# Value projections from a second, interleaved copy of the tokens, one transfer per chunk, and the second norm on ScalarE

## The chip, the cores and the metric

The kernel runs on one core of a Trainium2 chip. A core has a matrix engine (TensorE, PE in the profile; PEld is its weight load), a vector engine (VectorE, DVE), an activation engine (ScalarE, ACT), a general engine (GpSimd, POOL) and a sequencer that here issues nearly all DMA transfers (SyncE, SP). Each has its own instruction queue and works through it in order; semaphores join them. The metric is the device time of one execution in microseconds, as the median of several runs.

## The reference

The input is x with 32 sequences of 128 tokens of 128 features. First comes a cross-attention with 16 query heads of 8 features and 4 key/value heads, whose keys and values come from a context and whose scores get a bias from the time between tokens. Its result is added to x. Then x is normalized once and goes through six layers, whose result is added again. One layer is:

```
def attn_layer(x, Wqkv, qs, ksc, Wo):
    q, k, v = split(x @ Wqkv)            # 16 heads of 64 features
    q = l2norm(q) * qs;  k = l2norm(k) * ksc
    q, k = rotary(q), rotary(k)          # with a scale that depends on the position
    out = local_attention(q, k, v)       # windows of 32 tokens, each sees itself and the one before
    return out @ Wo

def ffn_layer(x, g, bln, W1, b1, W2, b2):
    xn = (x - mu) / sqrt(var + 1e-05) * g + bln
    a, gate = split(xn @ W1 + b1)
    return a * gelu(gate) @ W2 + b2

x = attn_layer(shift_tokens(x), ...) + x
x = ffn_layer(shift_tokens(x), ...) + x
```

`shift_tokens` replaces half of a token's features by those of the token before it. The "second norm" of the title is the layer norm that opens the feed-forward part; the norm of q and k is the L2 norm.

## The kernel before

**Units and groups.** A unit is one sequence in one layer: its 128 tokens lie on 128 partitions. Four sequences make a group (`GB = 4`), so a layer has 8 groups and 32 units, and six layers have 48 groups and 192 units. The groups of a layer do not depend on each other. Before the layers, `xgroup` and `xunit` compute the cross-attention, also in 8 groups of 4.

**What a group does.** `lgroup` transposes the shifted tokens of a group on TensorE (`ax`) and splits them into a rounded half and a remainder (`axh` on ScalarE, `axl` on VectorE), `xh` and `xl`. A product of two float32 matrices is made of three matmuls of such halves (`split3`, L435 to L437). Then come four units, and `ffn` ends the group.

**What a unit does.** For each of four chunks of 512 columns (q has two, k has two), `qk` projects, `sq` squares on ScalarE, `tab` multiplies by the rotary tables on VectorE (L793), `ss` sums the squares (L816), and `add` joins the rotary halves on GpSimd (L809). `newton` makes 1/sqrt of the 32 norms of a token: a maximum (`dmx`, L396), Ln and Exp on ScalarE, and one Newton step, which squares the estimate (L405) and multiplies twice (L409, L415), all `dnw` on VectorE. `mul` scales on GpSimd (L834), `tq` transposes, `evq` copies out (L838).

**The values.** Wv and Wo of a head are multiplied together beforehand (`mp`, `mh`, `ml` in `prep`), so the value projection `y` gives, for every head, 128 features that only have to be weighted and summed. `y` makes four chunks of 512 columns (4 heads of 128). `yt` copies a chunk out of PSUM (L851). The attention needs the keys of one window on 32 partitions, with the four windows and the heads along the free dimension, and one chunk's heads on their own 32 partitions. So for each chunk c, four transfers `dm` (L861), one per window u, move partitions 32u to 32u+31 of `yt` to partitions 32c to 32c+31 of `ysh`, columns 512u to 512u+511, 64 KB each. `av` (L913) multiplies with the transposed weights.

**The attention between.** `msk` writes the mask into PSUM (L884), `sc` adds the scores (L879), `mx` takes the negated row maximum (L892), `fold` adds it by a matmul (L893), `ex` exponentiates into `pr` (L895), `sm`, `rl` and `pl` normalize (L896 to L898), `pt` transposes blocks (L900).

**The second norm.** `ffn` adds the attention to x (L921), starts the token shift (`psh`, two transfers on SP, L752), takes mean and variance (`st`, `ag`), and `newton` makes 1/sqrt with its small operations on GpSimd. Then `xn` subtracts the mean and scales on VectorE, one instruction for each of the four sequences (L939). `ptn` transposes, and the gated feed-forward follows.

**The order of the work.** The order of each engine's queue is fixed when the program is built. Every operation is a `Sched.op` with a name; the table `COST` gives its engine, how long it holds the engine and when its result is ready; `LATER` adds to its priority (larger is later, in units of sequences), and `KEEP` says how many of the five shared PSUM banks must stay free behind it. `Sched.run` plays the program through with these durations: whenever an engine is free, it takes the ready operation with the smallest priority for which buffers can be had. Buffers come from pools of fixed size: for instance three `yt`, two `ysh`, two pairs `xh`/`xl`, three `pr`, and six `S` for the scores of the cross-attention, four of them borrowed from a `ysh` (`NS = 2` adds two). Options (`YD`, `ADD`, `XN`) choose between ways that are both written out; those taken move values inside SBUF, add on GpSimd and normalize on VectorE.

Of the kernel before, what the change touches and what calls it, by code (L numbers as in the profile page):

```python
# [8 lines left out]
F32 = mybir.dt.float32  # L9
# [7 lines left out]
P = 128  # L17
# [6 lines left out]
NYD = 6  # L24
NS = 2
YD = "sb"
ADD = "pool"
XN = "dve"
# [6 lines left out]
    mxs=("POOL", .26, .30), dmx=("DVE", .17, .25), dnw=("DVE", .18, .25), ln=("ACT", .2, .24), ep=("ACT", .2, .24), nw=("POOL", .31, .34),  # L35
    mul=("POOL", 1.08, 1.1), tq=("PE", .45, .70), evq=("ACT", .5, .62), evk=("ACT", .5, .62),
    y=("PE", .69, .90), yt=("ACT", .5, .62), dm=("SP", .62, 2.3), dw=("SP", .62, 3.5), dr=("SP", .62, 4.5),
# [3 lines left out]
    eps=("POOL", .22, .26), lnf=("ACT", .22, .21), epf=("ACT", .22, .21), nwf=("POOL", .3, .34), xn=("DVE", 1.05, 1.13), xn2=("POOL", 1.08, 1.1),  # L41
# [13 lines left out]
LATER = dict(y=3, xtr=0.75, ptn=1.5, fold=0.35, qk=-0.5, xsc=-1, axh=-1, evk=-0.25, ss=0.25, sc=0.25, sq=0.5, um=0.75,  # L55
    axl=-1.5, tq=1.25, xev=1.75, mul=0.75, mx=-1, evq1=-1.0, tab0=0.25, lnb=0.5, um1=-1, xpj=0.75, yt1=-1.5, rl1=0.75,
    dw=-1, gel=0.75, xn1=1, nw=-0.25, msk0=2, yt3=-1.25, ta3=0.5, pwm=-0.4, ag=0.25, tq0=1.5, pa0=-0.5, dnw=1, io=0.6,
    xnh=1.5, ep=-1.5, mx1=0.25, pt1=1.5, adda=0.9, ex1=1, gel1=0.35, dr=-0.15, ta1=1.5, msk=-1.5, adda1=2, xo=1.5,
    ta0=0.5, sm0=2.85, xsb=3, rl0=-1, mx0=-1, wve=-1.5, um0=0.25, evq2=-1.5, tq1=0.5, add3=2.1, xnl=2, gate1=0.5,
    nwf=1, xn2=0.25, add=1.5, lof=-1.5, yt2=0.5, wvp=0.75, ta=-0.5, xn=-0.5, ldw=-0.25, tq2=-0.25, res2=0.35, pt=0.25,  # L60
    xat=2)

KEEP = dict(qk=1, y=1, gate=1, pa=3, xtr=0, xpj=0, pv=1, td=1, xsc=0, wvp=2, mp=2, bip=2, sc0=0, ax=0, tq=0)
# [159 lines left out]
def body(ctx: ExitStack, tc: tile.TileContext, x, ctx_in, fside, mask_in, xWq, xWk, xWv, xWo, xtw,  # L223
         Wqkv, q_scale, k_scale, Wo, ln_g, ln_b, W1, b1, W2, b2, cst, x1d, y2d, out):
# [27 lines left out]
    if ADD == "dma":  # L252
        pool("rt", 5, [P, 1024])
    else:
        pool("rt", 10, [P, 512])
    pool("qT", 4, [P, 512])
    pool("ysh", 2, [P, 2048])
    pool("yt", 3, [P, 512], inorder=False)
    pool("pr", 3, [P, 512])
    pool("PT", 3, [P, 512])  # L260
    pool("xh", 2, [P, GB, P], F32R)
    pool("xl", 2, [P, GB, P], F32R)
    pool("nh", 1, [P, 512], F32R)
# [38 lines left out]

    S.pool("yd", [y2d[i] for i in range(y2d.shape[0])], False)
# [79 lines left out]
    def newton(names, pri, V, src, n, floor, eps, pool_, cols):  # L383
        v, y, t = [Buf(p) for p in pool_]

        def sl(b):
            return b.t[:, 0:n]
# [16 lines left out]
        def f3():  # L404
            e.tensor_tensor(sl(t), sl(y), sl(y), op=ALU.mult)  # L405
# [18 lines left out]
        S.op(names[3], f3, pri, [y], [t])  # L424
# [182 lines left out]
    def xgroup(g):  # L607
# [66 lines left out]
        if ADD == "dma":  # L674
            two = [Buf("rt", dt=F32R), Buf("rt", dt=F32R)]
            qs = [(two[t // 2], t % 2 * 512) for t in range(4)]
        else:
            qs = [(Buf("rt", dt=F32R), 0) for t in range(4)]
# [77 lines left out]
    def lgroup(l, g, w):  # L756
# [8 lines left out]
             [lo])  # L765
        for j in range(GB):
            unit(l, g, j, w, G, base + j)
        ffn(l, g, w, G, base + GB - 1)

    def unit(l, g, j, w, G, pri):  # L770
# [4 lines left out]

        hs = [(Buf("rt"), Buf("t")) for _ in range(2)] if ADD == "dma" else None

        def proj(c):
            pp, sq = Buf("pj"), Buf("sq")
            rt, t = hs[c // 2] if hs else (Buf("rt"), Buf("t"))  # L780
            o = c % 2 * 512 if hs else 0
            tok = Buf(None, 0) if hs else rt
            rts.append((rt, o, tok))
# [13 lines left out]
            def ta():  # L797
                nc.vector.tensor_tensor(rt.t[:, o:o + 512].rearrange("p (h d) -> p h d", d=64),
                                        pp.t.rearrange("p (h d) -> p h d", d=64), bc(tab.t[:, c // 2, 0], 8), op=ALU.mult)

            def tb():
                nc.vector.tensor_tensor(
                    t.t[:, o:o + 512].rearrange("p (h s d) -> p h s d", s=2, d=32)[:, :, ::-1, :],
                    pp.t.rearrange("p (h s d) -> p h s d", s=2, d=32),
                    bc(tab.t[:, c // 2, 1].rearrange("p (s d) -> p s d", s=2), 8), op=ALU.mult)

# [4 lines left out]
            if hs:  # L811
                S.op("ta", ta, pri, [pp, tab], [rt], also=[t], k=c)
                S.op("ta", tb, pri, [pp, tab], [t], k=c)
            else:
                S.op("tab", tab2, pri, [pp, tab], [t], k=c)
            S.op("ss", lambda: nc.vector.tensor_reduce(ss.t[:, c * 8:(c + 1) * 8], sq.t.rearrange("p (h d) -> p h d", d=64),  # L816
                                                       axis=AX.X, op=ALU.add), pri, [sq], [ss], k=c)
            if not hs:
                S.op("add", add, pri, [t], [rt], k=c)
            elif c % 2:  # L820
                S.op("adda", lambda: nc.gpsimd.dma_start(rt.t, t.t, accum_op=ALU.add), pri, [t, rt],
                     [rt, *(x[2] for x in rts[-2:])], k=c)
# [4 lines left out]
        for c in range(4):  # L827
            def tr(c):
                (rt, o, tok), pt, d = rts[c], Buf("pj"), Buf("qT")
                qT.append(d)  # L830

                def mul():
                    rv = rt.t[:, o:o + 512].rearrange("p (h d) -> p h d", d=64)
                    nc.gpsimd.tensor_tensor(rv, rv, rn.t[:, c * 8:(c + 1) * 8].unsqueeze(2).to_broadcast([P, 8, 64]),  # L834
                                            op=ALU.mult)
                S.op("mul", mul, pri, [tok, rn], [tok], also=[rt], k=c)
                S.op("tq", lambda: tr4(pt.t, [rt.t[:, o + k * P:o + (k + 1) * P] for k in range(4)]), pri, [tok], [pt], also=[rt, d], k=c)
                S.op("evq", lambda: nc.scalar.copy(d.t, pt.t), pri, [pt], [d], k=c)  # L838
            tr(c)
# [3 lines left out]
        yds = [Buf("yd"), Buf("yd")]  # L843
        for c in range(4):
            def yy(c):
                py, yt = Buf("pj"), Buf("yt")
                mh, ml = w["m"][c]
                yd = yds[c // 2]
                S.op("y", lambda: split3(py.t, (xh.t[:, j, :], xl.t[:, j, :]), (mh.t, ml.t)), pri, [xh, xl, mh, ml], [py],
                     also=ysh, k=c)  # L850
                S.op("yt", lambda: nc.scalar.copy(yt.t, py.t), pri, [py], [yt], k=c)  # L851
                if YD == "dram":
                    S.op("dw", lambda: nc.sync.dma_start(yd.t[:, c % 2], yt.t), pri, [yt], [yd], k=c)
                    if c % 2:
                        r = slice(32 * c - 32, 32 * c + 32)
                        S.op("dr", lambda: nc.sync.dma_start(
                            ysh[0].t[r].rearrange("p (u n) -> p u n", u=4),
                            yd.t.rearrange("u c i n -> (c i) u n")), pri, [yd], ysh, k=c)
                else:
                    for u in range(4):  # L860
                        S.op("dm", lambda u=u: nc.sync.dma_start(ysh[0].t[32 * c:32 * c + 32, u * 512:(u + 1) * 512],  # L861
                                                                 yt.t[32 * u:32 * u + 32, :]), pri, [yt], ysh, k=c)
            yy(c)
# [55 lines left out]
    def ffn(l, g, w, G, pri):  # L919
# [15 lines left out]

        if XN == "dve":
            def xnf():
# [128 lines left out]
```

## Time and profile before

| | us |
|---|---|
| median of 3 runs | 3436.73 (3434.03 to 3436.86) |
| profiled execution, device time | 3450.15 |
| its span, first to last instruction | 3448.4 |
| TensorE busy | 3113.7 |
| VectorE busy | 2917.7 |
| ScalarE busy | 2227.7 |
| GpSimd busy | 2413.6 |

The mean granted TensorE clock was 0.972. The profiled execution was 13.4 us longer than the median, so a sum made on the profile is compared with 3450.15 first. A row of the profile names the line of the kernel, the engine, the operation, the tiles written and read, how many there were and how long they were busy; a wait is named after the work that released it. Matmuls overlap in their pipeline, and their ends are modelled, so a busy TensorE may still have room. "SPq" is SyncE's queue, whose issues do not count as busy.

### The profile page before, as it was taken

To read this page: it belongs to the slowest core of one execution; us is meant where nothing else is said; L and a number is where in the kernel's file an instruction comes from. 1 tells how busy PE (TensorE), PEld (TensorE's weight loads), DVE (VectorE), ACT (ScalarE), POOL (GpSimd) and SP (SyncE) were. 2 spreads that over 40 slices of the span, in tenths; PEclk is the share of its full clock that TensorE was granted. 3 is DMA by queue.
4 is the path that set the end of the run, shared out by engine and by line. 5 is a ranking of instruction groups with operands and counts; after the bars stand their busy time and mean duration, and the time that the engine had idled before them with its cause. 6 is when DMAs were issued, how large, how long until landed. Compare 5 with 4: busy or idle time off the path is not lost.

```text
span 3448.4 us, 118846 instructions
## 1 busy us (share of the span) xinstructions
PE 3113.7 (90%) x47887; PEld 2404.7 (70%) x47887; DVE 2917.7 (85%) x6115; ACT 2227.7 (65%) x4415; POOL 2413.6 (70%) x2470
## 2 busy tenths in 40 slices
PE   8877899898799999799999999999999999999997
PEld 5554677676576777577777777777777777777775
DVE  5556998889678998779999889998899988899984
ACT  6766666666466666566766666666666667676664
POOL 6546877677557777656777767777677777677773
PEclk9998999999899999899999999999999999999998
DMA  4200132323133333233233333332332333333332
GB/s 105 58 13 10 48 78 67 76 68 90 41 87 74 74 80 76 56 92 74 69 79 79 87 77 78 75 82 68 91 80 69 79 74 85 79 75 87 82 78 71
DMA packets 253765, 251.06 MB, mean 73 GB/s; under 512 B 127486, under 2 KB 148258, under 8 KB 253218
## 3 DMA queue, kind: packets, MB, share of 16 engines
q1 hardware_dynamic: 252786, 243.12, 28.8%
q8 instruction: 380, 6.23, 0.9%
q14 instruction: 167, 1.37, 0.1%
q10 hardware_dynamic: 432, 0.34, 0.0%
HBM read 25.24 MB, written 4.19 MB: 9 GB/s over the span
## 4 chain that ended last, share of the span: by engine, by line
PE 34%; DVE 26%; DMA 11%; SPq 11%; ACT 10%; issue 6%; POOL 2%; ACTq 0%; POOLq 0%; DVEq 0%
SPq L861 10%; PE bank__68 L913 7%; DMA xt<-xt 2%; PE bank__66 L879 2%; PE bank__64 L441 1%; PE bank__67 L879 1%; PE bank__63 L441 1%; PE bank__61 L441 1%; PE bank__65 L441 1%; PE bank__63 L435 1%; PE bank__62 L435 1%; PE bank__62 L441 1%; PE bank__65 L435 1%; PE bank__61 L435 1%; PE bank__63 L436 1%
## 5 line engine op out<-in xcount | busy, mean ns | idle before, releaser
L884 ACT COPY bank__66<-mask 128x512 f32<-128x512 f32 x192 | 117.0, 610 | 5.7 <-PE bank__66 L362 4.4
L884 ACT COPY bank__67<-mask 128x512 f32<-128x512 f32 x192 | 116.5, 607 | 1.5 <-PE bank__67 L362 1.1
L724 ACT ACTIVATE ysh__88<-ysh__88 128x512 f32<-128x512 f32 x96 | 60.7, 634 | 57.0 <-POOL ysh__88 L722 56.9
L961 ACT ACT_TABLE_LOAD x48 | 61.6, 1283 | 0.9
L241 ACT ACT_TABLE_LOAD x48 | 61.6, 1283 | 0.9
L921 DVE TENSOR_TENSOR xt<-bank__68,xt 128x512 f32<-128x512 f32 x48 | 33.0, 687 | 16.7 <-PE bank__68 L913 16.5
L441 PE MATMUL bank__61<-cs,ysh__88 128*128 128x128 f32 x84 | 15.5, 315 | 10.2 <-ACT ysh__88 L724 10.2
L441 PE MATMUL bank__63<-cs,ysh__88 128*128 128x128 f32 x80 | 14.6, 312 | 10.8 <-ACT ysh__88 L724 10.5
L441 PEld LDWEIGHTS bank__63<-cs,ysh__88 128*128 128x128 f32 x80 | 9.9, 156 | 15.0 <-ACT ysh__88 L724 12.8
L441 PEld LDWEIGHTS bank__61<-cs,ysh__88 128*128 128x128 f32 x84 | 10.9, 160 | 13.6 <-ACT ysh__88 L724 12.2
L441 PE MATMUL bank__62<-cs,ysh__88 128*128 128x128 f32 x76 | 14.5, 324 | 5.6 <-ACT ysh__88 L724 5.4
L441 PE MATMUL bank__64<-cs,ysh__88 128*128 128x128 f32 x68 | 12.7, 318 | 7.6 <-ACT ysh__88 L724 7.5
L441 PE MATMUL bank__65<-cs,ysh__88 128*128 128x128 f32 x76 | 13.3, 302 | 6.4 <-ACT ysh__88 L724 6.1
L441 PEld LDWEIGHTS bank__62<-cs,ysh__88 128*128 128x128 f32 x76 | 10.7, 168 | 8.4 <-ACT ysh__88 L724 7.6
L695 DVE TENSOR_TENSOR xt<-bank__68,xt 128x512 f32<-128x512 f32 x8 | 5.5, 685 | 12.8 <-PE bank__68 L693 12.8
L441 PEld LDWEIGHTS bank__64<-cs,ysh__88 128*128 128x128 f32 x68 | 8.6, 159 | 10.9 <-ACT ysh__88 L724 10.2
L441 PEld LDWEIGHTS bank__65<-cs,ysh__88 128*128 128x128 f32 x76 | 9.5, 154 | 9.5 <-ACT ysh__88 L724 8.7
L991 POOL TENSOR_TENSOR raw__50988<-raw__50988,xt 128x512 f32<-128x512 f32 x1 | 1.3, 1262 | 19.7 <-DVE xt L984 19.7
L718 DVE CUSTOM_DVE_ANT_0 ysh__88<-bank__63,rt__2156 128x128 f32<-128x128 f32 x12 | 2.8, 287 | 12.7 <-ACT S__90 L727 6.2
L727 ACT COPY ysh__88<-bank__63 128x512 f32<-128x512 f32 x20 | 11.9, 597 | 1.8 <-PE bank__63 L441 1.6
L727 ACT COPY ysh__88<-bank__61 128x512 f32<-128x512 f32 x21 | 12.3, 586 | 1.2 <-PE bank__61 L441 1.1
L718 DVE CUSTOM_DVE_ANT_0 ysh__88<-bank__61,rt__2550 128x128 f32<-128x128 f32 x12 | 2.8, 288 | 12.1 <-ACT S__90 L727 5.6
(24588 smaller groups left out, 15904.7 us busy)
## 6 DMA issues: line engine op xcount, KB each, us to landing
xt<-xt SPq DMA_DIRECT2D x96, 112.0 KB, 2.5
xt<-in_x SPq DMA_DIRECT2D x16, 128.0 KB, 3.2
x_scratch<-xt SPq DMA_DIRECT2D x8, 256.0 KB, 3.0
xt<-xt SPq DMA_DIRECT2D x96, 15.0 KB, 2.2
stg__750<-in_L_ffn_Wo SPq DMA_DIRECT2D x1, 512.0 KB
stg__1904<-in_L_ffn_Wo SPq DMA_DIRECT2D x1, 512.0 KB
stg__20461<-in_L_ffn_Wo SPq DMA_DIRECT2D x1, 512.0 KB
stg__28190<-in_L_ffn_Wo SPq DMA_DIRECT2D x1, 512.0 KB
```

What stands on the lines that cost most here:

```text
L241: S.back = lambda: nc.scalar.preload_act_table_set("natural_log_exp_and_others")
L435: nc.tensor.matmul(pt, lh, rh, start=True, stop=False)
L436: nc.tensor.matmul(pt, lh, rl, start=False, stop=False)
L441: nc.tensor.transpose(dst[:, k * P:(k + 1) * P], srcs[k], ident)
L724: S.op("xex", lambda: nc.scalar.activation(sm.t, sm.t, AF.Exp), pri, [sm], [sm], table="E")
L727: S.op("xev", lambda: nc.scalar.copy(sm.t, pt.t), pri, [pt, sm], [sm])
L861: S.op("dm", lambda u=u: nc.sync.dma_start(ysh[0].t[32 * c:32 * c + 32, u * 512:(u + 1) * 512], yt.t[32 * u:32 * u + 32, :]), pri, [yt], y ...
L879: nc.tensor.matmul(s4[a][32 * c:32 * c + 32, half, wd, lo:64], q[r, c * P + 32 * wd:c * P + 32 * wd + 32], k[r, c * P + 32 * wd - 32 + lo: ...
L884: S.op("msk", lambda b=b: nc.scalar.copy(b.t, mask), pri, (), [b], k=a)
L913: nc.tensor.matmul(po.t[32 * wd:32 * wd + 32, j * P:(j + 1) * P], p5[a][:, half, wd, blk, :], ysh[0].t[:, u * 512 + h * P:u * 512 + (h + 1 ...
L921: S.op("res", lambda: nc.vector.tensor_tensor(xv(g), hv(po.t), xv(g), op=ALU.add), pri, [po, X[g]], [X[g]])
L961: S.op("gel", lambda: nc.scalar.activation(u.t[0:n], pg.t[0:n], AF.Gelu, bias=b1c.t[0:n, 1, i:i + 1]), pri, [pg, b1c], [u], table="G", k=i)
```

## The change

After `axh` and `axl` of a group, two more ScalarE copies (`xph`, `xpl`) write the same two halves into a second pair of buffers, `xq`, with the tokens in another order: token 32u + i goes to column 4i + u. The value projections take `xq` as their stationary operand in place of `xh` and `xl`, so that `yt` has token 32u + i on partition 4i + u. Four neighbouring partitions then hold what one partition of `ysh` needs, and one transfer of 256 KB moves a chunk, with 128 rows read and 32 rows written. The matmuls are as many as before and of the same shape.

The second norm is one ScalarE activation per sequence, with the scale 1/sqrt and a bias of minus mean times 1/sqrt, which a new small VectorE operation (`nmr`) writes over the mean. In the norm of q and k the square of the Newton step goes from VectorE to ScalarE (`ysq`).

To make room, `S` loses one buffer (`NS` is 1) and `pr` one (2 for 3); `xq` has two buffers, which is one pair. All of `LATER` is new, `KEEP` differs in `pa`, `xtr` and `ax`, and `COST` books `dmx`, `dnw`, `dm` and `xn` differently. The options and the branches that were not taken are deleted, and so is the DRAM scratch for values.

```diff
-NS = 2
+NS = 1
...
-    mxs=("POOL", .26, .30), dmx=("DVE", .17, .25), dnw=("DVE", .18, .25), ...
+    mxs=("POOL", .26, .30), dmx=("DVE", .32, .40), dnw=("DVE", .30, .38), ...
...
-    y=("PE", .69, .90), yt=("ACT", .5, .62), dm=("SP", .62, 2.3), ...
+    y=("PE", .69, .90), yt=("ACT", .5, .62), dm=("SP", .62, 3.2), xph=("ACT", .6, .7), xpl=("ACT", .6, .7), ...
...
-    ... xn=("DVE", 1.05, 1.13), ...
+    ... xn=("ACT", .92, 1.0), nmr=("DVE", .2, .28), ysq=("ACT", .2, .24), ...
...
-LATER = dict(y=3, xtr=0.75, ptn=1.5, fold=0.35, ...
+LATER = dict(y=3.25, xtr=-0.25, ptn=3, fold=0.75, ...
...
-KEEP = dict(qk=1, y=1, gate=1, pa=3, xtr=0, xpj=0, pv=1, td=1, xsc=0, wvp=2, mp=2, bip=2, sc0=0, ax=0, tq=0)
+KEEP = dict(qk=1, y=1, gate=1, pa=1, xtr=1, xpj=0, pv=1, td=1, xsc=0, wvp=2, mp=2, bip=2, sc0=0, tq=0)
...
-    pool("pr", 3, [P, 512])
+    pool("pr", 2, [P, 512])
...
+    pool("xq", 2, [P, GB, P], F32R)
...
         def f3():
-            e.tensor_tensor(sl(t), sl(y), sl(y), op=ALU.mult)
+            if small:
+                nc.scalar.activation(sl(t), sl(y), AF.Square)
+            else:
+                e.tensor_tensor(sl(t), sl(y), sl(y), op=ALU.mult)
...
+        G["xq"] = [Buf("xq"), Buf("xq")]
+
+        def weave(d, src):
+            nc.scalar.copy(d.t.rearrange("p b (i u) -> p b u i", u=4), src.t.bitcast(F32).rearrange("p b (u i) -> p b u i", u=4))
+        S.op("xph", lambda: weave(G["xq"][0], hi), pri, [hi], [G["xq"][0]])
+        S.op("xpl", lambda: weave(G["xq"][1], lo), pri, [lo], [G["xq"][1]])
...
-                S.op("y", lambda: split3(py.t, (xh.t[:, j, :], xl.t[:, j, :]), (mh.t, ml.t)), pri, [xh, xl, mh, ml], [py],
-                     also=ysh, k=c)
...
-                    for u in range(4):
-                        S.op("dm", lambda u=u: nc.sync.dma_start(ysh[0].t[32 * c:32 * c + 32, u * 512:(u + 1) * 512],
-                                                                 yt.t[32 * u:32 * u + 32, :]), pri, [yt], ysh, k=c)
+            S.op("y", lambda: split3(py.t, (xq[0].t[:, j, :], xq[1].t[:, j, :]), (mh.t, ml.t)), pri, [*xq, mh, ml], [py],
+                 also=ysh, k=c)
+            S.op("yt", lambda: nc.scalar.copy(yt.t, py.t), pri, [py], [yt], k=c)
+            S.op("dm", lambda: nc.sync.dma_start(ysh[0].t[32 * c:32 * c + 32, :], yt.t), pri, [yt], ysh, k=c)
...
-                for k in range(GB):
-                    nc.vector.tensor_scalar(xn.t[:, k * P:(k + 1) * P], xsg(g)[:, k], mv.t[:, k, 0:1], r.t[:, k:k + 1],
-                                            op0=ALU.subtract, op1=ALU.mult)
+        S.op("nmr", lambda: nc.vector.scalar_tensor_tensor(mv.t[:, :, 0], mv.t[:, :, 0], -1.0, r.t[:, 0:GB], op0=ALU.mult, op1=ALU.mult),
+             pri, [mv, r], [mv])
+
+        def xnf():
+            for k in range(GB):
+                nc.scalar.activation(xn.t[:, k * P:(k + 1) * P], xsg(g)[:, k], AF.Identity, bias=mv.t[:, k, 0:1],
+                                     scale=r.t[:, k:k + 1])
+        S.op("xn", xnf, pri, [X[g], XS[g], mv, r], [xn])
```

## The prediction

> **What bounds the kernel now.** I read the page first: busy times, then the chain of work that ended last.
>
> ```profile
> PE 3113.7 (90%) x47887; PEld 2404.7 (70%) x47887; DVE 2917.7 (85%) x6115; ACT 2227.7 (65%) x4415; POOL 2413.6 (70%) x2470
> ...
> PE 34%; DVE 26%; DMA 11%; SPq 11%; ACT 10%; issue 6%; POOL 2%; ACTq 0%; POOLq 0%; DVEq 0%
> ```
>
> TensorE (PE) is busy 3113.7 of 3448.4 us, so 334.7 us of idle time is the ceiling of any gain that leaves its work alone, as this change does. VectorE (DVE) at 85% is the second bound. The chain runs through all of them: no single wait sets the end.
>
> Next the busy times by stage (columns: stretch, length, then busy time of PE, weight loads, DVE, ACT, POOL, granted clock, DMA share, GB/s).
>
> ```profile
> 100.00:370.00 270.00, 222.01 (x1781) 149.06 (x1782) 169.98 (x994) 180.29 (x357) 151.67 (x172) 0.90 0.09 24
> ...
> 2900.00:3400.00 500.00, 466.48 (x7706) 367.73 (x7701) 444.56 (x795) 331.48 (x655) 368.64 (x366) 0.99 0.33 81
> ```
>
> The first is cross-attention: nothing is full. The second is the layer stage, six layers, 48 groups, 192 units, from 370 us on: PE 93% busy, DVE 89%, ACT 66%, at a granted clock of 0.99. One unit there takes about 15.5 us.
>
> Then the line that moves the values (L861): who waited for it, and what it issues.
>
> ```profile
>   PEld bank__68 L913: 56.6, 103
>   PE bank__68 L913: 48.2, 124
> ...
> DMA to landing us min/median/max: 1.9/2.0/4.0
> ```
>
> ```profile
> 910.04 2.44 SPq L861 DMA_DIRECT2D ysh__12554<-yt__12565  x4
> 912.57 2.44 SPq L861 DMA_DIRECT2D ysh__12538<-yt__12608  x4
> 915.11 2.43 SPq L861 DMA_DIRECT2D ysh__12538<-yt__12630  x4
> ```
>
> Four issues per chunk occupy SP for 2.44 us, four chunks per unit for 9.8 of some 15.5 us, and the last quarter lands 2.0 us after its issue. The matmuls of L913 then wait 48.2 us in all. ScalarE waits too: summed over all buffer numbers, its copies L851 stood 177 us in 148 waits between 900 and 3400 us for a `yt` buffer that SP had not emptied, with everything behind them on ACT's queue.
>
> Last, the normalization of the second norm (L939, 192 instructions) and VectorE's tiny ones of the q/k norm. The first two rows are L939's and L405's sums over the span (L405: 192 on DVE, then 64 on POOL); the others are a stretch of the timeline.
>
> ```profile
> 0.00:3448.40 3448.40, 131.05 (x192) 0.97 0.30 73
> ...
> 0.00:3448.40 3448.40, 79.20 (x192) 12.81 (x64) 0.97 0.30 73
> ```
>
> ```profile
> 895.93 1.26 POOL L809 TENSOR_TENSOR rt__12433<-t__12481 128x512 f32<-128x512 f32 x1
> ...
> 896.00 1.25 DVE L409 SCALAR_TENSOR_TENSOR rw__12489<-rv__12466,rw__12489 128x32 f32<-128x32 f32 x1
> ...
> 898.30 0.17 DVE L415 SCALAR_TENSOR_TENSOR ry__12476<-rw__12489,ry__12476 128x32 f32<-128x32 f32 x1
> ```
>
> A 128x32 operation lasts 1.25 us when a GpSimd addition runs beside it, and 0.17 us when none does. L939 is the same: instances of 335 ns and of up to 1351 ns, mean 131.05/192 = 683. The planner's table books a whole `xn` (four of them) at 1.05 us, and it takes 2.73.
>
> **The change, part by part.** The sum is made against the profiled execution, 3450.2 us (span 3448.4); the median of the runs is 13.4 us lower, and I subtract that at the end.
>
> *Values: 16 issues per unit become 4.* SP's issuing falls from 3072 x 0.59 = 1812 us to 768 x 0.59 = 453 us. No row shows a 256 KB transfer inside SBUF. Its landing is bounded by the 64 KB row (2.0 us) below, and above by that row's worst case plus the three issues that are saved, 4.0 + 1.8 = 5.8. The nearest row is the 256 KB store of L696, also cut into pieces by 16 engines: 3.0 us. I take 3.0. From the end of a `yt` copy to the landing of a chunk it was 3 x 0.59 + 0.59 + 2.0 = 4.4 us and becomes 0.59 + 3.0 = 3.6; for four chunks in a row it was 16 x 0.61 + 2.0 = 11.8 and becomes 4 x 0.61 + 3.0 = 5.4. Two views price this. Direct: PE's 48.2 us before L913, and 15 us in which PE waited for the copies L851 (its four rows, 5.5, 3.5, 3.4 and 2.4): 63 us. Chain: SPq is 11% of 3448 = 379 us, or 640 issues; DMA another 11%, some 150 landings of these values after the token shifts are taken out; so four issues precede each landing, one would remain, and 150 x (3 x 0.6 - 1.0) = 120 us would go. I take 75, as the chain has neighbours nearly as late. Ends: 0 (landing at 5.8) and 120.
>
> [...]
>
> *VectorE relieved.* `xn` leaves (131 us); of the small norm the square leaves (79 us); `nmr` comes, 48 x 0.31 = 15 us by L409's mean (60.32/192), between 0.15 and 1.25 each. Net 195 us less on an engine with 2918. With DVE on 26% of the chain that is 195 x 0.26 = 51 us. What backs it: PE's waits for the row maximum (L892), 53.1 + 5.7 us before L893, and for `xn`, 29.8 us. I take 50; ends 10 (cover elsewhere) and 89, which is all of those two waits.
>
> *ScalarE loaded.* Weaves: 96 x 0.61 (the 128x512 copy L884) = 59 us. The destination steps by 16 bytes, which no row shows; I bound it by 0.55 (L838, contiguous) and twice that, and take 0.61. `xn`: 192 at 9.47/32 = 0.30 us (L661, 128x128 with a bias) = 57. Squares of 128x32: 192 x 0.23 (L402, 57.98/256) = 44. Together 160 us on an engine that idles a third of the layer stage. With ACT on 10% of the chain: 16 us lost; ends 0 and 48, three times its share.
>
> *Buffers.* The woven copy has one pair for a group, where the plain one has two. The weave of the next group waits for the last value projection of this one. Value projections come in bursts, one per unit of 15.5 us, and the weave needs 1.2 us on ACT, so I cost it at nothing; the cover is the rest of the unit's work on PE, and without it see the rival. One of six score buffers of the cross-attention goes. PE waited there 40.6 us for the exponentials (the five groups of L441 after L724 in the page's list). With five buffers a head waits longer for one; 15 us lost, between 0 and 32 units x (1.02 + 0.63 + 0.56) = 71 us, one more pass through subtract, exponential and copy (L722, L724, L727) per unit. `pr` from three to two: three to five us of use, twice in 15.5 us; nothing.
>
> *Order.* All priorities are new, so every engine's order changes. Its one visible debt is two layer boundaries:
>
> ```profile
> 880.00:920.00 40.00, 28.32 (x237) 19.91 (x235) 29.98 (x48) 17.43 (x40) 31.49 (x28) 0.82 0.12 31
> ...
> 1410.00:1460.00 50.00, 32.95 (x292) 23.82 (x294) 35.10 (x60) 22.42 (x48) 36.08 (x34) 0.80 0.17 43
> ```
>
> PE idles 28.7 of 90 us there and the granted clock falls to 0.8, while SP has no values to move until 907 us: the next layer's weights are late. Against the 7% idle of the layer stage that is 22 us, and the clock costs about 15 more. Whether the new order repeats it can't be seen; I take -10, between -37 and +37.
>
> Sum: -75 - 50 + 16 + 15 - 10 = -104. Then 3450.2 - 104 = 3346, and 13.4 less against the median: **3333 us**, 3.0% faster. That is a third of PE's idle time. The removed branches of the options cost nothing; they were not taken.
>
> **The rivals.**
>
> *PE is already the bound (small gain).* Where a wait ends, PE finds the next one, and only the direct waits go: half of 63 us, 25 us of DVE's, against 31 us on the loss side: -26, so 3411. For it: PE 93% busy. Against it: DVE at 89% is nearly as full and gets lighter.
>
> *The queues loosen together (large gain).* If PE idles 3% instead of 7% in the layer stage (3030 us x 0.04 = 121 us), both late boundaries go (37) and ACT's freed queue pays for its load, with the cross-attention unhurt: some -190 with part of DVE's term, so 3247.
>
> *The single woven pair stalls value projections (slower).* Place: 47 group boundaries within the layers. The last projection of a group, two weaves, the copies queued before them on ACT, and only then the next projection. If PE's queue holds that projection next, PE stands 1.2 us for the weaves, 1.2 us for two copies ahead, 0.6 for the first matmuls to restart; and as the values then land 3.6 us later, L913 waits as well: up to 6 us. At 47 x 6 = 282 us against -104 the time is 3515. It decides from 104/47 = 2.2 us a boundary. Against it: projections are put back by three units and so have room. A poorly fitting new order would look the same.
>
> *The transfer does not get cheaper.* If an issue's cost grew with its pieces, one issue of 128 pieces would last as long as four of 32. L752 issues 112 rows in four pieces each and takes 0.67 us, L861 32 rows and takes 0.59, so I leave this almost no room; it would give 3333 + 75 = 3408, the case of the small gain.
>
> **How the numbers follow.** My forecast (3290 to 3380) has 0.46, the small gain (3385 to 3430) 0.20, the large one (3220 to 3290) 0.16, no change 0.03, slower 0.15. About 0.2% is what a measurement can tell from no change. Faster: 0.46 + 0.20 + 0.16 = 0.82; same 0.03; slower 0.15. The range drops 0.06 of the large gain and most of the slower case: 3235 to 3460.
>
> **What would show it.** Right: SP's rows one issue of about 0.6 us per chunk; PE's wait before the value matmuls under 20 us; ACT's waits for `yt` down from 177 us to under 60; DVE busy near 2720 us, ACT near 2390; PE near 95% in the layer stage. [...] Wrong: projections waiting for the weave at group boundaries; the cross-attention ending later than 370 us by more than 30; the granted clock falling at more than two layer boundaries; weaves of more than 1 us; `xn` on ACT holding back the exponentials.

## The result and the profile after

The kernel became slower: 3824.86 us as the median of four runs (3819.63 to 3828.77), against 3436.52 before on the same chip. The ratio is 1.1131 with a 95% interval of 1.1112 to 1.115. The forecast was 3333 us and its range ended at 3460, so both the sign and the size were missed.

The profiled execution has a span of 3826.7 us. These are the page's busy times and the shares of the chain that ended last, after the change.

```profile
PE 3155.4 (82%) x47887; PEld 2486.5 (65%) x47887; DVE 2762.1 (72%) x5779; ACT 2414.6 (63%) x4895; POOL 2410.4 (63%) x2470
...
PE 42%; DMA 31%; ACT 12%; DVE 7%; issue 6%; POOL 1%; SPq 0%; ACTq 0%; POOLq 0%; DVEq 0%
```

SP's queue has left the chain (it had 11%), and DMA went from 11% to 31%. TensorE's share fell from 90% to 82%. Its idle time is 3826.7 - 3155.4 = 671.3 us, where it was 334.7: 336.6 us more. The other 41.7 us of the longer span are TensorE's own busy time, with as many matmuls as before. The mean granted clock is 0.928, and it was 0.972.

By stage (columns: stretch, length, busy time of PE, weight loads, DVE, ACT and POOL, granted clock, DMA share, GB/s):

```profile
100.00:370.00 270.00, 225.75 (x1739) 149.89 (x1739) 163.12 (x985) 181.72 (x355) 152.26 (x175) 0.89 0.10 23
...
2900.00:3400.00 500.00, 418.93 (x6523) 335.54 (x6521) 369.47 (x646) 315.84 (x638) 317.39 (x313) 0.92 0.46 68
```

The cross-attention hardly moved. The layer stage did everything: in the same 500 us TensorE is busy 419 us for 466 before, at a clock of 0.92 for 0.99, and DMA's share is 0.46 for 0.33 while fewer bytes pass (68 GB/s for 81). Transfers that are longer with fewer bytes are the first sign.

The line that moves the values is now L829, and the value matmuls are at L881. Who waited for it:

```profile
  PE bank__68 L881: 387.9, 166
  PEld bank__68 L881: 117.5, 46
```

Before, these two rows were 48.2 and 56.6 us. In 166 places TensorE stood 2.3 us each for a value chunk. Summing TensorE's gaps in front of and inside the 56 value matmuls of each of the 192 units gives 412 us, against 56 us before: 174 units were held up by more than 0.3 us, the median unit by 2.1 us. The time lost between the medians is 388 us.

One such unit in the rows of SP and then of TensorE (start, duration, instruction; in brackets the idle time before it and what released it):

```profile
2006.83 0.63 SPq L829 DMA_DIRECT2D ysh__26428<-yt__26441  x1
2007.55 0.58 SPq L829 DMA_DIRECT2D ysh__26428<-yt__26513  x1
2009.70 0.55 SPq L829 DMA_DIRECT2D ysh__26428<-yt__26540  x1
2011.78 0.55 SPq L829 DMA_DIRECT2D ysh__26428<-yt__26563  x1
```

```profile
2014.85 0.40 PE L433 MATMUL bank__65<-wch__26232,xl__25570 128*128 128x512 f32 x1
2017.27 0.42 PE L881 MATMUL bank__68<-ysh__26428,PT__26516 128*32 128x128 f32 x8 [2.02 <-DMA ysh__26428<-yt__26563]
```

Each issue is one instruction of about 0.6 us, as the change says. But the last chunk is issued at 2011.78 and its matmuls begin at 2017.27, 5.5 us later. Over all units the median from the last issue to the first value matmul is 5.7 us. The planner's table books a landing 3.2 us after the start of the issue, and SP's queue for 0.62 us per chunk. TensorE's queue is in a fixed order, so the matmuls stand at its head where the table says that the values are there, and in the rows above TensorE stood still for 2.02 us until they came.

The trace's DMA packets and semaphore updates say why it takes so long. The completion packets of the four chunks lie at about 2009.5, 2011.6, 2013.6 and 2015.7 us. That is 2.05 us from one to the next, or 262144 B / 2.05 us = 128 GB/s, and the second chunk, issued 0.7 us behind the first, is done 2.1 us behind it. The first 81 of the first chunk's 128 packets of 2 KB take 81 to 95 ns each, nearly all packets of the later chunks 200 to 340 ns.

A chunk has landed with the last of its 16 semaphore updates, which release the matmuls. In this unit these come at 2011.2, 2014.5, 2016.6 and 2017.2 us, so each chunk landed more than a microsecond after most of its completion packets, and the first one took 4.3 us from its issue. Over all units the median landing of the four chunks is 4.3, 5.4, 5.9 and 5.5 us after the issue. The 19 chunks that had no other value transfer near them took 3.9 us (median), and no chunk took less than 3.8.

### The profile page after: what moved, and what is told of

Read it like the earlier page. It is cut to its first block, busy times and chain, and to the rows that moved or that the text cites. A ratio compares the mean times of both kernels' runs of the same rounds, so it can differ in the third digit from the quotient of the medians.

```text
span 3826.7 us, 115302 instructions
## 1 busy us (share of the span) xinstructions
PE 3155.4 (82%) x47887; PEld 2486.5 (65%) x47887; DVE 2762.1 (72%) x5779; ACT 2414.6 (63%) x4895; POOL 2410.4 (63%) x2470
## 4 chain that ended last, share of the span: by engine, by line
PE 42%; DMA 31%; ACT 12%; DVE 7%; issue 6%; POOL 1%; SPq 0%; ACTq 0%; POOLq 0%; DVEq 0%
PE bank__68 L881 13%; PE bank__66 L847 2%; PE bank__67 L847 2%; PE bank__63 L431 1%; PE bank__62 L437 1%; PE bank__62 L431 1%; PE bank__64 L431 1%; PE bank__63 L437 1%; PE bank__65 L431 1%; PE bank__61 L437 1%; PE bank__65 L437 1%; PE bank__61 L431 1%; PE bank__63 L433 1%; PE bank__63 L432 1%; PE bank__62 L432 1%
## 5 line engine op out<-in xcount | busy, mean ns | idle before, releaser
L716 ACT ACTIVATE ysh__88<-ysh__88 128x512 f32<-128x512 f32 x112 | 70.9, 633 | 57.5 <-POOL ysh__88 L714 57.3
L889 DVE TENSOR_TENSOR xt<-bank__68,xt 128x512 f32<-128x512 f32 x48 | 33.0, 688 | 100.2 <-PE bank__68 L881 100.1
L437 PE MATMUL bank__61<-cs,ysh__88 128*128 128x128 f32 x104 | 19.3, 315 | 9.1 <-ACT ysh__88 L716 9.0
L437 PE MATMUL bank__65<-cs,ysh__88 128*128 128x128 f32 x108 | 21.4, 332 | 5.7 <-ACT ysh__88 L716 5.5
L437 PE MATMUL bank__62<-cs,ysh__88 128*128 128x128 f32 x96 | 19.7, 341 | 6.0 <-ACT ysh__88 L716 5.9
L437 PEld LDWEIGHTS bank__65<-cs,ysh__88 128*128 128x128 f32 x108 | 15.4, 171 | 10.4 <-ACT ysh__88 L716 9.3
L437 PEld LDWEIGHTS bank__61<-cs,ysh__88 128*128 128x128 f32 x104 | 13.2, 159 | 13.5 <-ACT ysh__88 L716 12.5
L437 PEld LDWEIGHTS bank__62<-cs,ysh__88 128*128 128x128 f32 x96 | 13.9, 174 | 10.5 <-ACT ysh__88 L716 8.9
L437 PE MATMUL bank__63<-cs,ysh__88 128*128 128x128 f32 x72 | 13.8, 324 | 6.9 <-ACT ysh__88 L716 6.9
L437 PE MATMUL bank__64<-cs,ysh__88 128*128 128x128 f32 x68 | 12.9, 321 | 6.1 <-ACT ysh__88 L716 6.0
L687 DVE TENSOR_TENSOR xt<-bank__68,xt 128x512 f32<-128x512 f32 x8 | 5.5, 690 | 16.9 <-PE bank__68 L685 16.9
L719 ACT COPY ysh__88<-bank__62 128x512 f32<-128x512 f32 x24 | 14.0, 585 | 4.7 <-PE bank__62 L437 2.7
L719 ACT COPY ysh__88<-bank__65 128x512 f32<-128x512 f32 x27 | 15.9, 589 | 1.5 <-PE bank__65 L437 1.4
L719 ACT COPY ysh__88<-bank__61 128x512 f32<-128x512 f32 x26 | 15.3, 590 | 1.9 <-PE bank__61 L437 1.3
L949 DVE TENSOR_TENSOR xt<-bank__61,xt 128x512 f32<-128x512 f32 x12 | 8.2, 686 | 11.5 <-PE bank__61 L945 11.5
L437 PEld LDWEIGHTS bank__63<-cs,ysh__88 128*128 128x128 f32 x72 | 9.2, 161 | 10.4 <-ACT ysh__88 L716 10.2
L437 PEld LDWEIGHTS bank__64<-cs,ysh__88 128*128 128x128 f32 x68 | 9.1, 163 | 10.5 <-ACT ysh__88 L716 8.5
```

What stands on the lines that cost most here:

```text
L437: nc.tensor.transpose(dst[:, k * P:(k + 1) * P], srcs[k], ident)
L716: S.op("xex", lambda: nc.scalar.activation(sm.t, sm.t, AF.Exp), pri, [sm], [sm], table="E")
L719: S.op("xev", lambda: nc.scalar.copy(sm.t, pt.t), pri, [pt, sm], [sm])
L889: S.op("res", lambda: nc.vector.tensor_tensor(xv(g), hv(po.t), xv(g), op=ALU.add), pri, [po, X[g]], [X[g]])
```

## The experiments

The theory after the result was: *late landing*. The transfer drains slowly, the table does not know it, and TensorE's in-order queue pays in every unit. Its rival was *the new order*: the new priorities, or the work moved to ScalarE, fit badly, and the waits for the values only show it. All kernels on one table, the gaps being TensorE's in front of and inside the value matmuls, worked out from each trace as above, and the packet the median 2 KB packet of SP's hardware queue (q1) after 400 us. A ratio is to the kernel before as it was measured beside that run: 3441 us beside e1 to e4, 3439 beside e5 to e8, 3424 beside e9 to e11.

| kernel | median us | ratio to before | PE busy, idle us | gaps us | packet ns |
|---|---|---|---|---|---|
| before | 3436.5 | | 3113.7, 334.7 | 56 | 140 |
| after | 3824.9 | 1.1131 | 3155.4, 671.3 | 412 | 241 |
| e1, to 128 partitions | 3277.6 | 0.9529 | 3010.5, 260.4 | 18 | 84 |
| e9, to 32 partitions four apart | 3289.7 | 0.9615 | 3002.6, 286.7 | 34 | 84 |
| e5, to 64 neighbouring partitions | 3780.6 | 1.0994 | 3173.0, 608.1 | 345 | 233 |
| e2, four transfers, new order | 4102.3 | 1.1927 | 3408.0, 694.7 | 448 | 82 |
| e3, after, booked (2.1, 5.5) | 3383.2 | 0.9836 | 3018.0, 358.6 | 57 | 211 |
| e7, after, booked (0.62, 5.5) | 3459.1 | 1.0061 | 3059.6, 394.3 | 69 | 211 |
| e4, before with the new priorities | 3469.3 | 1.0079 | 3120.6, 346.4 | 68 | 140 |
| e6, before with the norm part alone | 3393.3 | 0.9877 | 3091.5, 288.1 | 74 | 140 |
| e8, after, all bookings | 3368.9 | 0.9795 | 3037.7, 332.3 | 44 | 202 |
| e10, e8 without the norm part | 3500.8 | 1.0239 | 3081.1, 409.0 | 49 | 216 |
| e11, e8 with other priorities | 3293.5 | 0.9625 | 3011.4, 287.2 | 14 | 204 |

**e1: the same transfer, to all partitions.** Same size, source, number and planned order; the edit changes only where the 256 KB go, and so leaves out the regrouping by windows. One thing follows from it: a group of value matmuls now reads what one chunk wrote, so the first of them waits for the first chunk alone. e9 below keeps the wait for all four chunks.

```diff
-ysh[0].t[32 * c:32 * c + 32, :], yt.t
+ysh[0].t[:, 512 * c:512 * c + 512], yt.t
```

> The changed kernel, order and all, but a chunk's transfer of 256 KB writes all 128 partitions (512 columns each) and no longer 32. It leaves out the regrouping by windows, so the values stand in the wrong places; every instruction is there. Theory 'landing': the transfer into 32 partitions lands some 5.7 us after its issue, where the planner books 3.2, and PE's queue holds the value matmuls too early; a wide destination lands in about 3 us, PE's waits for these transfers (505 us over PE and its weight loads) fall under 100, and the time is 3400 to 3480 us. Rival 'order': the new priorities are bad as a whole; the time stays above 3700.

Measured: 3277.62 us, ratio 0.9529 (0.9482 to 0.9576), below the expected range. The median landing of a chunk is 2.4 us. Who waited for L829 in e1:

```profile
  PEld bank__68 L881: 14.5, 23
  PE bank__68 L881: 8.2, 16
```

The 387.9 us of waits are 8.2, and with nothing else changed the kernel is 547 us shorter than after. The late landing therefore carries the whole loss, and more: the rest of the change, when the values come in time, is worth 4.7% less time than before. The new order as the cause falls.

**e2: the same order, with four transfers per chunk as before.**

```diff
-lambda: nc.sync.dma_start(ysh[0].t[32 * c:32 * c + 32, :], yt.t)
+lambda: [nc.sync.dma_start(ysh[0].t[32 * c:32 * c + 32, u * 512:(u + 1) * 512],
+    yt.t.rearrange("(i u) n -> u i n", u=4)[u]) for u in range(4)]
```

> The changed kernel with the same order, but each chunk moves in four transfers of 64 KB (every fourth partition of the woven chunk to 32 partitions), as before the change. Theory 'landing, set by the 32 partitions written': SP takes 2.4 us per chunk, four chunks land about 11.8 us after the first issue against 5.8 + 5.7 = 11.5 us now, so the time hardly moves: 3750 to 3900 us. If the single large transfer as such is slow, the waits go and the time is 3400 to 3550. Rival 'order': above 3700 too, so this run doesn't tell order from landing; e1 does.

Measured: 4102.28 us, 1.1927 (1.188 to 1.1973), above the expectation. SP's rows of one unit in e2:

```profile
2000.02 2.38 SPq L829 DMA_DIRECT2D ysh__25801<-yt__25812  x4
2002.50 2.46 SPq L829 DMA_DIRECT2D ysh__25801<-yt__25820  x4
2005.06 2.45 SPq L829 DMA_DIRECT2D ysh__25801<-yt__25839  x4
2007.60 2.46 SPq L829 DMA_DIRECT2D ysh__25801<-yt__25876  x4
```

SP is held 2.45 us per chunk where the table books 0.62, and the last issue comes 11.0 us after the first (median over the units), in after 6.0. The last transfer lands in 2.1 us, and yet the values are later: 11.0 + 2.1 = 13.1 us from a unit's first issue, against 6.0 + 5.5 = 11.5 in after. By this estimate e2 is 192 x 1.6 = 307 us behind after, and it is 277 us. Only 36 us of it show as gaps. The rest stands as TensorE's busy time (3408.0 us for 3155.4), in which the ends of matmuls are modelled, and the value matmuls alone account for it (780.8 us for 504.8). So one transfer does relieve SP, as the change says; an order built on one transfer per chunk was not fed in time by four.

The packets are quick here (82 ns) although they go to the same 32 partitions. SP's pace, 64 KB per 0.61 us or 107 GB/s, is under the 128 GB/s at which these partitions drained in after; that this is the reason was not shown. In before, at the same pace and to the same partitions, a packet took 140 ns; there the 32 source partitions were neighbours, and here they lie four apart.

**e3 and e7: the same program, with other bookings.** Only the entry for the transfer (queue held, landing after its start) differs; the planner then orders the queues anew.

```diff
-dm=("SP", .62, 3.2)
+dm=("SP", 2.1, 5.5)      # e3
+dm=("SP", .62, 5.5)      # e7
```

> The changed kernel with one number of the planner's table changed: a chunk's transfer is booked at 2.1 us of the queue and 5.5 us to its landing instead of 0.62 and 3.2. All operations are the same, their order is planned anew. 'Landing': PE's waits for the transfers fall under 150 us and the time is 3420 to 3550 us. 'Order': the priorities are the same, and the time stays above 3700.

> As e3, but only the landing is booked anew (5.5 us), the queue still at 0.62 us per transfer. If the landing alone was the error, the time is that of e3 within 1%, 3350 to 3417 us. If the rate at which chunks can follow each other (2.05 us apart in the packets) matters as well, the queue's debt comes back as waits: 3430 to 3600 us.

Measured: e3 3383.23 us, 0.9836 (0.9787 to 0.9885), below the expected range; e7 3459.14 us, 1.0061 (1.0035 to 1.0087), within it. Who waited for L829 in e3, and then the landing of L829 in e7:

```profile
  PE bank__68 L881: 16.9, 17
  PEld bank__68 L881: 4.2, 5
```

```profile
DMA to landing us min/median/max: 3.8/4.7/9.4
```

The packets are still slow (211 ns in both), and the landings are late. In e3 the value matmuls begin 6.6 us after the last issue (median), and TensorE hardly waits for the values any more, because these matmuls stand further back in its queue. Two numbers in a table are worth 442 us. The landing alone recovers 366 of them. The other 76 us come with the rate, 2.1 us between two chunks; only 12 us of that difference lie in front of the value matmuls (69 against 57 us of gaps). Where the rest went in the re-planned order was not settled.

**e4: the old kernel with the new priorities.** `LATER` and `KEEP` are taken from after, and nothing else.

```diff
-LATER = dict(y=3, xtr=0.75, ptn=1.5, fold=0.35, ...
+LATER = dict(y=3.25, xtr=-0.25, ptn=3, fold=0.75, ...
-KEEP = dict(qk=1, y=1, gate=1, pa=3, xtr=0, ..., ax=0, tq=0)
+KEEP = dict(qk=1, y=1, gate=1, pa=1, xtr=1, ..., tq=0)
```

> The kernel before with the tables LATER and KEEP of the changed kernel, nothing else. 'Landing': the priorities are no worse than the old ones by more than 2%, 3370 to 3505 us. 'Order': they carry most of the loss, 3650 us or more.

Measured: 3469.3 us, 1.0079 (1.0056 to 1.0102). The priorities cost the old kernel 0.8%, not 11%. This lies within the expected range of *late landing*.

**e5 and e9: is it the number of partitions?** Both again change only the destination of after's transfer: 64 neighbouring partitions in e5, and in e9 32 partitions as in after, but four apart.

```diff
-ysh[0].t[32 * c:32 * c + 32, :]
+ysh[0].t[64 * (c % 2):64 * (c % 2) + 64, 1024 * (c // 2):1024 * (c // 2) + 1024]   # e5
+ysh[0].t[c::4, :]                                                                # e9
```

> The changed kernel, order and all, with a chunk's 256 KB written to 64 partitions (1024 columns each), between the 32 of the change and the 128 of e1. The values stand in the wrong places. If the landing is set by how many partitions are written, a 2 KB packet, about 300 ns with 32 and 80 ns with 128, takes about 150 ns; the landing comes near the booked 3.2 us, PE's waits for the transfers stay under 120 us and the time is 3280 to 3400 us. If 32 partitions are a cliff of another kind and not a rate, the time is that of e1 within 0.5%, 3262 to 3294, or that of the changed kernel, 3825.

> The changed kernel, order and all, with a chunk written to 32 partitions that lie four apart instead of side by side; size, count of partitions and pieces are those of the change. The values stand in the wrong places. [...] If the number of partitions counts, the time stays at 3780 to 3830.

Measured: e5 3780.61 us, 1.0994 (1.0958 to 1.103), e9 3289.74 us, 0.9615 (0.9582 to 0.9649). Who waited for L829, first in e5, then in e9:

```profile
  PE bank__68 L881: 332.2, 176
  PEld bank__68 L881: 305.4, 128
```

```profile
  PE bank__68 L881: 17.6, 22
  PEld bank__68 L881: 5.6, 7
```

Both leave out the regrouping. In e9, as in after, the first value matmul waits for all four chunks. Twice as many neighbouring partitions leave a 2 KB packet at 233 ns (241 in after), so e5's expectation that the number counts fell; as many partitions as in after, but spread, bring it to 84, and a chunk's landing from 5.4 to 2.4 us (medians). For the same bytes the DMA engines worked 0.416 x 3826.7 = 1592 us in after and 0.216 x 3289.3 = 710 us in e9. These are the rows of SP's queue (packets, MB, share of 16 engines) in after and in e9:

```profile
q1 hardware_dynamic: 215922, 242.97, 41.6%
```

```profile
q1 hardware_dynamic: 215922, 242.97, 21.6%
```

With one transfer of 256 KB per chunk, what counted in these runs is which partitions are written, not how many: a 2 KB packet takes 241 ns to 32 neighbours, 233 to 64 neighbours, 84 to 32 that lie four apart and 84 to all 128. e9's 3289.74 us is far below the 3780 to 3830 us that stood for the number of partitions. Why neighbouring partitions drained more slowly no run shows.

In after, a chunk's heads stand on 32 neighbouring partitions for the matmuls of L881. A regrouping by windows that writes to spread partitions, with the weights brought into the same places, was not tried.

**e6: the norm part alone, in the old kernel.** The second norm and the square go to ScalarE, with `nmr` and the changed bookings of `dmx`, `dnw` and `xn`; values, buffers and priorities stay.

```diff
-            e.tensor_tensor(sl(t), sl(y), sl(y), op=ALU.mult)
+            if small:
+                nc.scalar.activation(sl(t), sl(y), AF.Square)
+            else:
+                e.tensor_tensor(sl(t), sl(y), sl(y), op=ALU.mult)
...
-                    nc.vector.tensor_scalar(xn.t[:, k * P:(k + 1) * P], xsg(g)[:, k], mv.t[:, k, 0:1], r.t[:, k:k + 1],
-                                            op0=ALU.subtract, op1=ALU.mult)
+                    nc.scalar.activation(xn.t[:, k * P:(k + 1) * P], xsg(g)[:, k], AF.Identity, bias=mv.t[:, k, 0:1],
+                                         scale=r.t[:, k:k + 1])
```

> The kernel before with the second part of the change alone: the second norm and the square of the Newton step on ScalarE, with the bookings of these operations as in the changed kernel; values, buffers and priorities stay as before. The forecast gave this part about -50 us for VectorE and some +10 us for ScalarE (its weaves left out): 3385 to 3410. Rival: VectorE's relief is covered, and ScalarE's load costs as much: 3425 to 3460.

Measured: 3393.29 us, 0.9877 (0.9847 to 0.9906), 46 us less than before in the same runs. Its page:

```profile
PE 3091.5 (91%) x47887; PEld 2394.5 (71%) x47887; DVE 2756.1 (82%) x5779; ACT 2317.7 (69%) x4799; POOL 2413.9 (71%) x2470
```

This half of the change is worth what it was priced at, in the old order.

**e8, e10 and e11: the other bookings, the other half, and new priorities.** e8 books the transfer as e3 does, the two copies and the norm as after's trace has them, and lets the value projections come a little earlier. e10 is e8 with norm and square back on VectorE. e11 is e8 with eleven more priorities changed (its expectation says about two dozen; the table differs in eleven).

```diff
-dm=("SP", .62, 3.2), xph=("ACT", .6, .7), xpl=("ACT", .6, .7)
+dm=("SP", 2.1, 5.5), xph=("ACT", .95, 1.05), xpl=("ACT", .95, 1.05)
...
-xn=("ACT", .92, 1.0)
+xn=("ACT", 1.6, 1.7)        # e8, e11
+xn=("DVE", 2.7, 2.8)        # e10, with both operations as before
...
-LATER = dict(y=3.25, ...
+LATER = dict(y=2.5, ...
...
-    mx1=-0.75, nwf=-0.25, pv=2.0, xat=2.25, xph=1
+    mx1=-2.25, nwf=0.75, pv=0.5, xat=3.25, xph=0.5, dnw=0.25, ln=-0.5, mul3=0.5, pa1=2.0, qk2=-1.0, tq2=1.75   # e11
```

> The changed kernel with four bookings set to what its trace shows: the transfer 2.1 and 5.5 us, the weaves 0.95 us, the second norm on ScalarE 1.6 us, and the value projections put back by 2.5 units and not 3.25. It is to beat the kernel before and e3: 3330 to 3383 us. If ScalarE's wrong bookings cost nothing, it stays within 0.5% of e3, 3366 to 3400.

> e8 with the second norm and the square back on VectorE, the norm booked at the 2.7 us that it took before the change. Woven copy, single transfers, buffers and priorities stay. If the two halves of the change add up, e8's 3369 us lose the 46 us that e6 gained: 3400 to 3430. If ScalarE, loaded by the weaves, had made the norms' move worthless, 3355 to 3380.

> e8 with about two dozen of the priorities moved so that the planner's own schedule, with the bookings set to the trace, ends 1.6% earlier. All operations are those of e8. If the schedule now describes the chip, the time falls by about as much, 3300 to 3345 us; if not, it stays at 3350 to 3400.

Measured: e8 3368.92 us, 0.9795 (0.9773 to 0.9817); e10 3500.8 us, 1.0239 (1.0208 to 1.0269); e11 3293.52 us, 0.9625 (0.9596 to 0.9654). e8 lies in both of its expected ranges and within e3's interval, so it does not tell what ScalarE's wrong bookings cost. If the halves multiplied, e10 would be at 0.9795 / 0.9877 = 0.992; it is 3% above that, and 71 us above the expected range. Its gaps at the value matmuls are only 49 us, so the values are not what it waits for. With both operations back on VectorE the planner makes another order under the same priorities, and what in it costs the time stays open. e11 does the whole work of after, with after's slow transfers (204 ns a packet), and it beats both kernels, 3.75% under before. TensorE is busy 91% of it, and the value matmuls wait 14 us in all. Whether the old kernel would gain from a retuning too was not tried, so this lead need not all be the change's.

## Why the prediction was wrong, point by point

**The step that failed: "Values: 16 issues become 4", priced at -75 with ends 0 and -120.** Its half on SP came true: one issue of 0.55 to 0.63 us per chunk, and SP out of the chain. The other half, a landing of 3.0 us, did not. The row that it was taken from is a store out of SBUF; the transfer here writes 32 neighbouring partitions, one chunk behind another. A chunk with no other near it landed in 3.9 us, and the last of a unit's four in 5.5. That is close to the upper bound of 5.8, by luck: the bound adds a 64 KB row's worst case and three issues, and what the runs show is a slow drain (128 GB/s).

The bound also got the wrong price. A landing at 5.8 was called no gain. That compares two chains of transfers as if the matmuls came whenever the values are there. The queues do not allow that: they are in a fixed order, built with a landing of 3.2 us. What lands later than that is due in each of 192 units. With the bound itself that is an estimated (5.8 - 3.2) x 192 = 499 us of waits, with the measured landing (5.5 - 3.2) x 192 = 442 us, and TensorE's gaps are 412. The lower end of the term was a loss of over 400 us, not 0.

**The missing view** was the change in the table itself, `dm` from (.62, 2.3) to (.62, 3.2). It stood in the diff and was read as a number, not as a promise that every queue is built on. e1, e9 and e3 show it from both sides: quick packets with the old promise (3278, 3290), or slow packets with a true one (3383).

**A chunk by itself was late as well.** The chunks with no other near them landed in 3.9 us, 0.7 us beyond the booking. Even that, at 192 units, would be an estimated 0.7 x 192 = 134 us of waits, where the prediction let the term fall to zero. That the place of the written partitions changes the rate (241 ns a packet in after, 84 in e9) was not in the prediction.

**The slower rival had the right queue and the wrong cause.** It put TensorE behind the single woven pair at 47 boundaries. From 900 us to 3800 us TensorE waited 2.2 us in all for the copies into that pair, and 315 us for values. Its side remark, that values which land late make the value matmuls wait as well, was the mechanism, in 174 of 192 units. Its sum has a slip as well: 3333 + 282 is 3615 us, not 3515. So its chance of 0.15 was met for another reason than the one given.

**VectorE relieved and ScalarE loaded** were right together. The norm part alone gave 46 us (e6); by the terms it is -50 for VectorE plus 10 of the 16 for ScalarE (101 of its 160 us), so -40. The 1.25 us that the prediction gives a 128x32 operation beside a GpSimd addition is near the worst case: in before, those of L405, L409 and L415 that began beside one took 0.13 to 1.31 us (medians by line 0.33 to 0.52), and those with GpSimd idle 0.13 to 0.19. VectorE's busy time fell by 156 us and not by 195, since its other rows grew; ScalarE's rose by 187 and not by 160. Two of ScalarE's rows were mis-sized. These are the sums over the span of after for the copies of L762 and for the norm of L909 (ScalarE's busy time, then clock, DMA share and GB/s):

```profile
0.00:3826.70 3826.70, 100.79 (x96) 0.93 0.43 66
```

```profile
0.00:3826.70 3826.70, 79.27 (x192) 0.93 0.43 66
```

A copy into the woven order takes 1.05 us of ScalarE's busy time, 1.17 from its start to its end (means; taken 0.61, bound 1.1; more than 1 us was among the signs of being wrong), a sequence of the norm 0.41 us (taken 0.30). The square of 45.14/192 = 0.235 us was right (0.23). The three come to 225 us, more than the 187, partly because neighbouring ScalarE rows overlap in the trace (a pair of the copies began at 419.3 and 420.2 us and lasted 1.12 us each).

**Buffers.** One score buffer less was priced at 15 us. The cross-attention's end moved from 368 to 375 us, by the first value matmuls of the layers, and in e1 to 369. The waits for its exponentials are 33.8 us for 40.6. So the term was 0 to 7 us.

**Order**, -10 between -37 and +37: the priorities by themselves cost the old kernel 28 us (e4), within the bounds but with the other sign; what they are worth in the new kernel was not separated. The two late layer boundaries are gone in after: outside the value matmuls, no 50 us of its layers hold more than 7.1 us of TensorE's gaps, where the worst in before held 14.7.

**The signs given in advance.** TensorE's wait before the value matmuls was to be under 20 us and was 388, which says by itself which step fell. ScalarE's waits for `yt` were to fall from 177 us to under 60; they are 113.5 us in 96 waits (between 900 and 3800 us), each ended by the landing of a value transfer. VectorE at 2762 us (near 2720) and ScalarE at 2415 (near 2390) fit. TensorE was to be near 95% in the layer stage and is at 84%.

**The forecast without the late landing** had the right sign: e1 is 4.7% and e9 3.85% under before, beyond the -3.0% of the sum, towards the large gain of the rivals (3247 us).

## What to carry to other kernels

In a program whose queues are ordered beforehand, do not price a transfer that lands later than booked as a lost gain: here it was a stall of TensorE in 174 of 192 units, 412 us in all. Price it as lateness times repetitions, (5.5 - 3.2) x 192 = 442 us here, and book both the landing and the rate from a trace in which the transfers follow one another. When transfers were merged here, the saved issues came as counted and the landing did not (5.5 us for 3.0); look at the landings by the semaphore, and at which partitions the destination occupies, not only at how many (32 neighbours 241 ns a packet, 32 four apart 84). When a bound of a term is worked out, ask what the other engines were promised before calling the bound zero.

## What the runs showed of the hardware that was not expected

- 256 KB into 32 neighbouring partitions drained at 128 GB/s in after, with 2 KB packets of 241 ns at the median; into 32 partitions four apart (e9), or into all 128 (e1), the same packets took 84 ns. 64 neighbours (e5): 233 ns.
- The end of a chunk's packets was not its landing. In the unit shown, the first 81 packets go at 81 to 95 ns also towards the slow destination, and the first chunk's completion packets are done by 2009.5 us, but its semaphore updates come at 2010.8 to 2011.2. Towards spread partitions (e9, a chunk issued at 2000.88 us) the completion packets are done by 2002.95 us, and the updates come at 2003.1 to 2003.2.
- The stalls came with more than their own length. From e1 to after TensorE's idle time grows by 410.9 us and its busy time by 144.9, for the same matmuls, while the mean granted clock falls from 0.981 to 0.928. Of the busy time, 110.3 us lie in the value matmuls, which come right behind the stall (L881, first in e1, then in after: busy time of PE and of weight loads, clock, DMA share, GB/s):

```profile
0.00:3270.90 3270.90, 394.48 (x10752) 331.92 (x10752) 0.98 0.22 77
```

```profile
0.00:3826.70 3826.70, 504.75 (x10752) 428.92 (x10752) 0.93 0.43 66
```

  In after, the value matmuls of 87 units ran for most of their time at a granted clock of 0.5 and were busy 3.36 us a unit (mean); those of the other 105 units were busy 2.02 us, about as in e1 (2.06). The 87 had stood 3.0 us before (median), the others 1.5. So some 87 x 1.34 = 117 us go with the lower clock, an estimate from these rows.
- ScalarE's copy of 128x512 into `xq` (L762), whose neighbouring results are written 16 bytes apart, lasted 1.17 us from start to end (mean of 96); the copy of the same size and type that writes them next to each other (L755) lasted 0.61 us (mean of 48). The second reads PSUM and the first SBUF.
- One part of a chunk was late while a packet of another queue ran. In the unit shown above, a packet of 16 KB on queue q8, which the profile lists as "instruction", took 1.7 us from 2009.5 us on, and the last of the 16 updates of the second and third chunk came 1.3 and 1.4 us behind the other fifteen; for the last chunk, for which the matmuls wait, it was 0.2 us. Over the whole of after, 127 chunks had a last update more than 0.5 us behind the rest, and 112 of these had such a packet in their time. That the packet is the reason is the author's inference; the trace here does not name the DMA engine.
